# Scans that begin from a constant, and the fifth tile's inputs ahead of the second tile's product, in a selective-scan hybrid block

## The chip, the cores and the metric

The kernel runs on one core of one Trainium2 chip, as one launch. The metric is the device time of that launch in microseconds (us). Engines go by their names in the profile: PE is TensorE, DVE is VectorE, ACT is ScalarE, POOL is GpSimd, SP is SyncE, which issues the DMAs. A difference of some 0.2% is about what a measurement of this kernel can tell from none.

## The reference

The input is x, 8 images of 96 channels, 64 x 64. Layer 0 is a state-space block with a convolutional side: layer norm, a projection to 192 channels and a gate z, a depthwise convolution, then four selective scans (row-wise and column-wise windows, each forwards and backwards) with 16 states to a channel, summed, normed, gated and projected, and a channel-attention part. Layer 1 is attention without softmax and a feed-forward network with fp8 rounding. The part that the change touches is the scan, over l = 4096 positions for each image, direction k, channel d and state n:

```python
def step(hst, inp):
    u_i, dt_i, b_i, c_i = inp
    dA = jnp.exp(dt_i[..., None] * A)
    hst = dA * hst + (dt_i * u_i)[..., None] * b_i[:, :, None, :]
    y = jnp.einsum('bkdn,bkn->bkd', hst, c_i)
    return (hst, y)
h0 = jnp.zeros((bb, k, d, n), u.dtype)
_, ys = lax.scan(step, h0, (u_t, dt_t, b_t, c_t))
return ys.transpose(1, 2, 3, 0) + D[None, :, :, None] * u
```

The names: dA is the decay, dt_i * u_i * b_i the input, hst the state, c_i what the state is multiplied with.

## The kernel before

**Units and tiles.** The scans are cut into 256 units: 8 images x 4 sequences (`order` 0 to 3, a window direction and a scan direction) x 8 chunks of T = 512 positions. A unit is worked in 24 slots, six tiles of G = 4 slots (`TILES`: state group g of 0, 1, channel block j of 0, 1, 2). A slot is one scan over 128 partitions (64 channels x 2 halves of the states) and 512 positions. The state at the end of a chunk goes on to the next unit of its sequence through a column of the tile `carry` (24 columns, one for each slot); the first unit of a sequence (`u.start`) begins from 0.0.

**What a slot runs.** ScalarE makes the decay of the slot two ahead, exp(delta * a), into one of four PSUM banks "da" (`decays(q + 2)`, line 1123). GpSimd has made the inputs of a whole tile beforehand, b * du, 128 x 2048, into a buffer "hb" of six (`inputs`, line 998). VectorE scans (line 1195), with `col`, a pointer to a column of `carry`, as the initial value, or with the constant 0.0. Then comes the product with C, in one of two ways:

- a *banked* slot writes its scan over the decay in PSUM, VectorE makes the product behind the next scan (line 1201) into hb, and ScalarE copies the last state from PSUM to `carry` (line 1202);
- in the other slots the scan writes over the inputs in hb, ScalarE copies the last states of the tile in one instruction (line 1207), and GpSimd makes the product of those slots in place (`outputs`, line 1004).

`BANKED` says how many slots of each of the six tiles are banked: (4, 0, 4, 0, 4, 2), or (4, 0, 4, 0, 4, 3) in image 0 and in the second to fourth sequence of the other images. So tiles 0, 2 and 4 are VectorE's, tiles 1 and 3 GpSimd's, and tile 5 is shared.

PE sums the products over the states by matmuls with `halves` (`sums`, line 1024), ScalarE empties the sums (`gather`), and SP stores them.

**The order.** All engines run in program order, and the order is written out by hand: `plan` says in which slot each step is issued (`put(slot, f, ...)`). Of those the change touches `inputs(u, n + 2)` at slot 4n + 1 (for n of 4 and 5 the next unit's first two tiles), and `sums` of tiles 0 and 1 from slot 13 on. Beside them stand `outputs` of tile 5 of the unit before (slot 0), of tile 1 (8) and tile 3 (16); `step_sizes`, which makes delta and delta * u (its products on GpSimd at slots 12 and 16, line 980); `spread`, `states`, `fetched_dt`, `fetched_u` and `fetched_pair`, which are DMAs on SP. The loads of b and c (`states`, two buffers each) come at slots 7, 10, 15 and 20. In every slot `advance` also runs one step of the side streams: the front part of the next image and the back part of the image before, with their own matmuls, evictions on ScalarE, table loads (line 275) and products on VectorE (lines 450, 465, 653 and others).

**Waits.** A decay needs its bank back: from the product and the carry copy of a banked slot, or from the scan of another. hb of tile n comes back when PE has summed it. `outputs` waits for its tile's scans and for their carry copy, since it overwrites them. `inputs` waits for b, du and a buffer.

Of the kernel before, what the change touches and what calls it, by code (L numbers as in the profile page):

```python
# [9 lines left out]
F32 = mybir.dt.float32  # L10
# [3 lines left out]
ALU = mybir.AluOpType  # L14
# [8 lines left out]
T = 512  # L23
NC = L // T
G = 4
# [5 lines left out]
SPREAD = 5  # L31
HB = 6

BANKED = ((4, 0, 4, 0, 4, 2), (4, 0, 4, 0, 4, 3))

HOLD = 3
LAND = 11
# [6 lines left out]
def kernel(ctx: ExitStack, tc: tile.TileContext, a, out):  # L44
# [8 lines left out]
    nc = tc.nc  # L53
    P = 128
# [8 lines left out]
    def bank(tag, name):  # L63
        return psum.tile([P, T], F32, tag=tag, name=name, bufs=BANKS[tag])
# [630 lines left out]
    def in_turn(stages, k, settle):  # L695

        for stage, cs in stages:
            yield from stage(k, cs)
            if settle:
                yield from settled()  # L700
# [12 lines left out]
    def drained(*streams, beside=()):  # L713
        while any(s.on for s in streams):
            tick()
            for s in (*streams, *beside):
                s.run()

    def all_issued():
        drained(Stream(iter((HOLD + 1,))))  # L720
# [12 lines left out]
    units, images = [], []  # L733
    for b in range(out.shape[0]):

        s = {"b": b, "done": set(), "live": b + 1 == out.shape[0], "pairs": (1, 0) if b else (0, 1)}
        images.append(s)
        for order, (pair, back) in enumerate((p, k) for p in s["pairs"] for k in range(2)):
            for i in range(NC):
                u = Unit()  # L740
                u.s, u.pair, u.back, u.k = s, pair, back, pair + 2 * back
                u.c, u.start = (NC - 1 - i if back else i), i == 0
                u.order, u.new, u.i = order, (order, i) == (0, 0), len(units)
                u.bc, u.hb, u.delta, u.du, u.p = {}, {}, {}, {}, {}
                u.banked = BANKED[int(b == 0 or u.i % 32 >= NC)]
                units.append(u)

    TILES = [(g, j) for g in range(2) for j in range(3)]
# [3 lines left out]
    first = front(0, images[0])  # L752
# [170 lines left out]
    sp = scan_pool.enter_context(tc.tile_pool(name="scan", bufs=2))  # L923
# [76 lines left out]
    def outputs(u, n):  # L1000

        lo = u.banked[n]
        hb = u.hb[n][:, lo:, :]
        nc.gpsimd.tensor_tensor(hb, hb, u.bc[1, TILES[n][0]][:, lo:, :], ALU.mult)  # L1004

# [51 lines left out]
    def plan(u, last, nxt, third, fourth):  # L1057

        at = [[] for _ in range(24)]

        def put(slot, f, *args):
            at[slot].append((f, args))

        if last:
            put(0, outputs, last, 5)
            for m in range(2):
                put(m, sums, last, (3, 4), 2 + m)
            for m in range(2):
                put(3 + m, sums, last, (5,), m)
            put(3, gather, last, 0)  # L1070
            put(7, states, u, 1, 1)
            put(7, gather, last, 1)
        for n in range(6):
            to = (u, n + 2) if n < 4 else (nxt, n - 4)
            if to[0]:
                put(4 * n + 1, inputs, *to)
        if third and u.i % 2:
            put(16, step_sizes, (nxt, third), 5)
        put(8, outputs, u, 1)
        put(16, outputs, u, 3)  # L1080
        for m in range(4):
            put(13 + m, sums, u, (0, 1), m)
            if m < 2:
                put(18 + m, sums, u, (2,), m)
                put(22 + m, sums, u, (3, 4), m)
        put(18, before, u)
        if nxt:
            put(0, spread, nxt, 0, (0, 1))
            put(1, spread, nxt, 1, (0, 1))
            put(10, states, nxt, 0, 0)  # L1090
            put(15, states, nxt, 1, 0)
            put(20, states, nxt, 0, 1)
            if u.i % 2 == 0:
                put(15, spread, nxt, 0, (2,))
                put(16, spread, nxt, 1, (2,))
        if third:
            if third.i < NC:
                put(0, fetched_dt, third)
            put(5, fetched_u, third)
            for i, slot in enumerate((6, 8, 9, 10, 11, 12)):  # L1100
                put(slot, step_sizes, (third,), i)
            if u.i % 2:
                for i, slot in enumerate((9, 11, 12, 13, 15)):
                    put(slot, step_sizes, (nxt, third), i)
                put(17, spread, nxt, 0, (2,))
                put(18, spread, nxt, 1, (2,))
            elif u.i + 3 < len(units):
                put(21, fetched_pair, third, units[u.i + 3])
        if fourth and fourth.i >= NC:
            put(14, fetched_dt, fourth)  # L1110
        return at

    def at_index(i):
        return units[i] if 0 <= i < len(units) else None

    def decays(q):

        if q >= 24 * len(units):
            return
        u, (n, m) = units[q // 24], divmod(q % 24, G)  # L1120
        g, j = TILES[n]
        da[q] = bank("da", "da")
        nc.scalar.activation(  # L1123
            da[q], u.delta[j], AF.Exp, scale=a_neg[:, u.k, j, g * G + m : g * G + m + 1]
        )

    da, kept, side, carry, product = {}, [], [], None, None
    for u in units[:2]:
        fetched_dt(u)
    fetched_u(units[0])  # L1130
# [10 lines left out]
    inputs(units[0], 0)  # L1141
    inputs(units[0], 1)
    decays(0)
    decays(1)
    for i in range(6):
        step_sizes(units[1:2], i)

    def advance(n):

        tick()  # L1150
        for st in side[:]:
            st.run()

    for u in units:
        last, nxt, third, fourth = (at_index(u.i + d) for d in (-1, 1, 2, 3))
        if u.new:
            drained(*side)
            b = u.s["b"]
            side = []
            if b == 0:  # L1160
                half_done.pace = 1.0
                side += [Stream(behind(kit_2, pairs[3:])), half_done]
            else:
                side.append(Stream(chain((SETTLE,), in_turn(back_end(b - 1, last.s), kit_b, False))))
            if b == 0:
                pass
            elif b + 1 < out.shape[0]:
                side.append(Stream(in_turn(front(b + 1, images[b + 1]), kit_f, True), PACE))
            else:
                final = back_end(b, u.s)  # L1170
                last_kit = back_kit(None, "f0", True, kit_f)
                side.append(Stream(final[0][0](last_kit, range(1, NC)[::-1])))
        if u.i == pairs[2] - 2:
            drained(half_done, beside=side[:1])
            side[1] = Stream(in_turn(front(1, images[1]), kit_f, True), PACE * (1 - u.i / 32))
        if u.i == pairs[3] - 2:
            drained(side[0])
        if fourth and fourth.new:
            drained(*side[-1:])
            all_issued()  # L1180
        if u.start:
            carry = sp.tile([P, 24], F32, tag="carry", name="carry")
        todo = plan(u, last, nxt, third, fourth)
        for slot in range(24):
            n, m = divmod(slot, G)
            g, j = TILES[n]
            q, hb, first_at = 24 * u.i + slot, u.hb[n], 0 if u.back else T - 1
            col = carry[:, 8 * j + g * G + m : 8 * j + g * G + m + 1]
            while kept:
                kept.pop(0)()  # L1190
            decays(q + 2)
            d = da.pop(q)
            banked = m < u.banked[n]
            dd, x = (d[:, ::-1], hb[:, m, ::-1]) if u.back else (d, hb[:, m, :])
            nc.vector.tensor_tensor_scan(dd if banked else x, dd, x, 0.0 if u.start else col, ALU.mult, ALU.add)  # L1195
            if product:
                product()
                product = None
            if banked:
                def product(d=d, x=hb[:, m, :], c=u.bc[1, g][:, m, :], col=col, at=first_at):  # L1200
                    nc.vector.tensor_tensor(x, d, c, ALU.mult)  # L1201
                    kept.append(lambda: nc.scalar.copy(col, d[:, at : at + 1]))  # L1202
            elif m == G - 1:
                lo = 8 * j + g * G
                kept.append(
                    lambda c=carry[:, lo + u.banked[n] : lo + G].unsqueeze(2), h=hb[:, u.banked[n] :, :], at=first_at:
                    nc.scalar.copy(c, h[:, :, at : at + 1])  # L1207
                )
            for f, args in todo[slot]:
                f(*args)  # L1210
            place[0] = slot
            advance(slot)
    place[0] = None
    if product:
        product()
# [87 lines left out]
```

## Time and profile before

| what | value |
|---|---|
| time, median of 3 runs (lowest to highest) | 10,763.39 us (10,757.55 to 10,774.28) |
| the profiled execution: time; its span | 10,764.72 us; 10,763.0 us |
| instructions | 97,608 |
| busy in the span, PE; DVE; ACT; POOL | 8,423.7; 10,158.1; 7,397.8; 10,118.0 us |
| mean granted TensorE clock | 0.841 |
| DMA | 2,253 MB, mean 209 GB/s, 0.87 of the 16 engines busy during the scans |
| inputs on POOL, L998, 128 x 2048 | 1536, mean 4,546 ns |
| products on POOL, L1004: 2048; 1024; 512 elements wide | 512, 4,539 ns; 56, 2,362 ns; 200, 1,291 ns |
| decays on ACT, L1123 | 6144, mean 689 ns |
| carry copies on ACT, L1202; L1207 | 3784, 157 ns; 768, 195 ns |

How to read it: a busy time is a union, so where instructions of one engine overlap (the next one's start with the last one's end) the sum of their durations is more than the busy time, and the distance from start to start says what one costs. The scans run from 176 to 10,537 us of the span; what lies before is the front part of image 0, and what lies behind is the back part of the last image. In a group of the profile the columns are line, engine, operation, output <- inputs with shapes and type, count, busy us, mean ns of one, and the engine's idle time just before them with what ended most of it.

### The profile page before, as it was taken

To read this page: it belongs to the slowest core of one execution; us is meant where nothing else is said; L and a number is where in the kernel's file an instruction comes from. 1 tells how busy PE (TensorE), PEld (TensorE's weight loads), DVE (VectorE), ACT (ScalarE), POOL (GpSimd) and SP (SyncE) were. 2 spreads that over 40 slices of the span, in tenths; PEclk is the share of its full clock that TensorE was granted. 3 is DMA by queue.
4 is the path that set the end of the run, shared out by engine and by line. 5 is a ranking of instruction groups with operands and counts; after the bars stand their busy time and mean duration, and the time that the engine had idled before them with its cause. 6 is when DMAs were issued, how large, how long until landed. Compare 5 with 4: busy or idle time off the path is not lost. (4 is left out here: it accounts for less than half of the span.)

```text
span 10763.0 us, 97608 instructions
## 1 busy us (share of the span) xinstructions
PE 8423.7 (78%) x23270; PEld 2274.2 (21%) x23270; DVE 10158.1 (94%) x11126; ACT 7397.8 (69%) x15154; POOL 10118.0 (94%) x2782
## 2 busy tenths in 40 slices
PE   7777668886788867888688886888768887677677
PEld 2121112221122211222122221222112221111112
DVE  3999999999999999999999999999999999999993
ACT  4666666777676776777767776677766767666674
POOL 3999999999999999999999999999999999999991
PEclk8888788987889878998789887898778987778788
DMA  6888888998889988898888988889888898888883
GB/s 148 208 205 209 200 209 214 226 226 200 215 216 227 227 193 220 216 231 219 201 218 214 237 212 202 217 220 237 198 211 218 219 235 200 202 203 210 208 214 94
DMA packets 1095381, 2253.29 MB, mean 209 GB/s; under 512 B 435993, under 2 KB 436698, under 8 KB 963731
## 3 DMA queue, kind: packets, MB, share of 16 engines
q1 hardware_dynamic: 1094803, 2247.05, 84.5%
q8 instruction: 184, 3.01, 0.1%
q14 instruction: 394, 3.23, 0.1%
HBM read 1507.14 MB, written 336.69 MB: 171 GB/s over the span
## 5 line engine op out<-in xcount | busy, mean ns | idle before, releaser
L998 POOL TENSOR_TENSOR hb<-b,du 128x2048 f32<-128x2048 f32 x1536 | 6952.6, 4546 | 6.1 <-DMA du<-ua 5.2
L1024 PE MATMUL p<-hb,halves 128*64 128x512 f32 x12288 | 3713.8, 707 | 1053.0 <-POOL hb L1004 562.6
L1123 ACT ACTIVATE da<-delta,w_a_logs 128x512 f32<-128x512 f32 x6144 | 4164.3, 689 | 541.5 <-DVE hb L1195 447.5
L1195 DVE TENSOR_TENSOR_SCAN da<-da,carry,hb 128x512 f32<-128x512 f32 x3311 | 4164.0, 1274 | 90.7 <-ACT carry L1202 37.0
L1004 POOL TENSOR_TENSOR hb<-hb,c 128x2048 f32<-128x2048 f32 (+2 forms) x768 | 2714.3, 3534 | 222.3 <-ACT carry L1207 203.0
L1195 DVE TENSOR_TENSOR_SCAN hb<-da,carry,hb 128x512 f32<-128x512 f32 x2065 | 2547.0, 1265 | 1.8
L1201 DVE TENSOR_TENSOR hb<-da,c 128x512 f32<-128x512 f32 x3784 | 2534.0, 670 | 1.8 <-DMA c<-xd 0.9
L1202 ACT COPY carry<-da 128x1 f32<-128x1 f32 x3784 | 593.8, 157 | 2054.5 <-DVE hb L1201 2045.1
L1024 PEld LDWEIGHTS p<-hb,halves 128*64 128x64 f32 x12288 | 904.8, 157 | 3697.8 <-issue 1876.0
L313 PE MATMUL conv<-f0im,taps 97*128 97x512 f32 (+1 forms) x2088 | 867.7, 655 | 37.2 <-ACT f0pre L369 32.2
L1195 DVE TENSOR_TENSOR_SCAN da<-da,hb 128x512 f32<-128x512 f32 x473 | 566.1, 1214 | 28.0 <-POOL hb L998 26.6
L963 PE MATMUL dt<-dts,dt_w 7*128 7x512 f32 (+1 forms) x1024 | 485.9, 742 | 92.3 <-ACT carry L1207 36.2
L980 POOL TENSOR_TENSOR ua<-nat,ua 128x512 f32<-128x512 f32 x256 | 329.9, 1289 | 170.9 <-DVE nat L977 161.8
L313 PEld LDWEIGHTS conv<-f0im,taps 97*128 97x128 f32 (+1 forms) x2088 | 256.4, 173 | 588.2 <-issue 508.8
L1207 ACT COPY carry<-hb 128x4 f32<-128x4 f32 (+2 forms) x768 | 149.7, 195 | 302.1 <-DVE hb L1195 293.7
L1195 DVE TENSOR_TENSOR_SCAN hb<-da,hb 128x512 f32<-128x512 f32 x295 | 346.8, 1205 | 1.7 <-ACT carry L1202 1.7
L259 PE MATMUL var<-f1e,ones_c 96*96 96x512 f32 x350 | 225.6, 731 | 121.8 <-ACT f1e L256 68.5
L253 PE MATMUL ctr<-f1e,cen_c 96*96 96x512 f32 x402 | 218.1, 649 | 86.1 <-ACT f1e L592 34.2
L977 DVE SCALAR_TENSOR_TENSOR nat<-dt,nat 128x512 f32<-128x512 f32 x384 | 258.0, 672 | 17.9 <-ACT nat L975 12.7
L975 ACT ACTIVATE nat<-nat,one 128x512 f32<-128x512 f32 x384 | 271.8, 708 | 0.1
L497 PE MATMUL cab<-f1im,cab_w 97*32 97x512 f32 x1044 | 256.0, 603 | 12.5 <-DMA f1im<-xld 7.1
L275 ACT ACT_TABLE_LOAD x193 | 247.6, 1283 | 4.1 <-PEq L1292 0.8
(430 smaller groups left out, 7586.0 us busy)
## 6 DMA issues: line engine op xcount, KB each, us to landing
b<-xd SPq DMA_DIRECT2D x1024, 512.0 KB
c<-xd SPq DMA_DIRECT2D x1024, 512.0 KB
delta<-nat SPq DMA_DIRECT2D x1536, 128.0 KB
du<-ua SPq DMA_DIRECT2D x1024, 128.0 KB
y<-yt SPq DMA_DIRECT2D x512, 256.0 KB
u<-y SPq DMA_DIRECT2D x384, 256.0 KB
ua<-u SPq DMA_DIRECT2D x256, 256.0 KB
du<-ub SPq DMA_DIRECT2D x512, 128.0 KB
```

The costliest lines, as they stand in the source:

```text
L313: nc.tensor.matmul(ps, taps[:, t, lo : lo + n], im[:, r0 + dy : r0 + dy + 8, dx : dx + HW], start=t == 0, stop=t == 8,)
L963: nc.tensor.matmul(ps, dt_w.rearrange("r j d -> r (j d)")[32 * w.k : 32 * w.k + R + 1, d], w.dts, start=True, stop=True)
L975: nc.scalar.activation(u.nat, u.nat, AF.Ln, bias=one)
L977: nc.vector.scalar_tensor_tensor(u.nat, u.ps, 0.0, u.nat, ALU.max, ALU.add)
L980: nc.gpsimd.tensor_tensor(x, u.nat, x, ALU.mult)
L998: nc.gpsimd.tensor_tensor(hb, u.bc[0, g], u.du[j].unsqueeze(1).to_broadcast([P, G, T]), ALU.mult)
L1004: nc.gpsimd.tensor_tensor(hb, hb, u.bc[1, TILES[n][0]][:, lo:, :], ALU.mult)
L1024: nc.tensor.matmul(ps, halves, u.hb[n][:, i, :], start=TILES[n][0] == 0 and m == 0, stop=False, skip_group_check=True)
L1123: nc.scalar.activation(da[q], u.delta[j], AF.Exp, scale=a_neg[:, u.k, j, g * G + m : g * G + m + 1])
L1195: nc.vector.tensor_tensor_scan(dd if banked else x, dd, x, 0.0 if u.start else col, ALU.mult, ALU.add)
L1201: nc.vector.tensor_tensor(x, d, c, ALU.mult)
L1202: kept.append(lambda: nc.scalar.copy(col, d[:, at : at + 1]))
```

## The change

- The initial value of a scan is a constant: 0.0 at the start of a sequence as before, and 1.0 otherwise. In its place ScalarE multiplies the first decay of each slot (the last column in a backward sequence) by the carried state, right behind the exponential that made the decay. With an initial value of 1.0 the scan's first state is then dA * carry + input. The tile `carry` hangs on the unit (`u.carry`), since the decays of a unit's first two slots are made while the unit before still runs.
- `BANKED` becomes (4, 0, 4, 0, 4, 3) and (4, 0, 4, 0, 4, 4); the second now holds only in the even units of those that had it. Where all of tile 5 is banked, `outputs` has nothing to do for it, and nor has the tile's carry copy of line 1207.
- The slots of `inputs` go from 1, 5, 9, 13, 17, 21 to 1, 5, 6, 11, 18, 21, so tile 4's inputs stand ahead of tile 1's `outputs` in GpSimd's order; the sums of tiles 0 and 1 start at slot 14 instead of 13.

```diff
--- before.py
+++ after.py
@@ -31,7 +31,7 @@
 SPREAD = 5
 HB = 6
 
-BANKED = ((4, 0, 4, 0, 4, 2), (4, 0, 4, 0, 4, 3))
+BANKED = ((4, 0, 4, 0, 4, 3), (4, 0, 4, 0, 4, 4))
 
 HOLD = 3
 LAND = 11
@@ -742,7 +742,7 @@
                 u.c, u.start = (NC - 1 - i if back else i), i == 0
                 u.order, u.new, u.i = order, (order, i) == (0, 0), len(units)
                 u.bc, u.hb, u.delta, u.du, u.p = {}, {}, {}, {}, {}
-                u.banked = BANKED[int(b == 0 or u.i % 32 >= NC)]
+                u.banked = BANKED[int((b == 0 or u.i % 32 >= NC) and u.i % 2 == 0)]
                 units.append(u)
 
     TILES = [(g, j) for g in range(2) for j in range(3)]
@@ -1000,6 +1000,8 @@
     def outputs(u, n):
 
         lo = u.banked[n]
+        if lo == G:
+            return
         hb = u.hb[n][:, lo:, :]
         nc.gpsimd.tensor_tensor(hb, hb, u.bc[1, TILES[n][0]][:, lo:, :], ALU.mult)
 
@@ -1073,13 +1075,13 @@
         for n in range(6):
             to = (u, n + 2) if n < 4 else (nxt, n - 4)
             if to[0]:
-                put(4 * n + 1, inputs, *to)
+                put((1, 5, 6, 11, 18, 21)[n], inputs, *to)
         if third and u.i % 2:
             put(16, step_sizes, (nxt, third), 5)
         put(8, outputs, u, 1)
         put(16, outputs, u, 3)
         for m in range(4):
-            put(13 + m, sums, u, (0, 1), m)
+            put(14 + m, sums, u, (0, 1), m)
             if m < 2:
                 put(18 + m, sums, u, (2,), m)
                 put(22 + m, sums, u, (3, 4), m)
@@ -1123,8 +1125,15 @@
         nc.scalar.activation(
             da[q], u.delta[j], AF.Exp, scale=a_neg[:, u.k, j, g * G + m : g * G + m + 1]
         )
-
-    da, kept, side, carry, product = {}, [], [], None, None
+        if not u.start:
+            u.carry = units[u.i - 1].carry
+            first = da[q][:, T - 1 : T] if u.back else da[q][:, 0:1]
+            nc.scalar.mul(first, first, state(u.carry, j, g, m))
+
+    def state(carry, j, g, m, n=1):
+        return carry[:, 8 * j + g * G + m : 8 * j + g * G + m + n]
+
+    da, kept, side, product = {}, [], [], None
     for u in units[:2]:
         fetched_dt(u)
     fetched_u(units[0])
@@ -1179,31 +1188,30 @@
             drained(*side[-1:])
             all_issued()
         if u.start:
-            carry = sp.tile([P, 24], F32, tag="carry", name="carry")
+            u.carry = sp.tile([P, 24], F32, tag="carry", name="carry")
         todo = plan(u, last, nxt, third, fourth)
         for slot in range(24):
             n, m = divmod(slot, G)
             g, j = TILES[n]
             q, hb, first_at = 24 * u.i + slot, u.hb[n], 0 if u.back else T - 1
-            col = carry[:, 8 * j + g * G + m : 8 * j + g * G + m + 1]
             while kept:
                 kept.pop(0)()
             decays(q + 2)
             d = da.pop(q)
             banked = m < u.banked[n]
             dd, x = (d[:, ::-1], hb[:, m, ::-1]) if u.back else (d, hb[:, m, :])
-            nc.vector.tensor_tensor_scan(dd if banked else x, dd, x, 0.0 if u.start else col, ALU.mult, ALU.add)
+            nc.vector.tensor_tensor_scan(dd if banked else x, dd, x, 0.0 if u.start else 1.0, ALU.mult, ALU.add)
             if product:
                 product()
                 product = None
             if banked:
-                def product(d=d, x=hb[:, m, :], c=u.bc[1, g][:, m, :], col=col, at=first_at):
+                def product(d=d, x=hb[:, m, :], c=u.bc[1, g][:, m, :], col=state(u.carry, j, g, m), at=first_at):
                     nc.vector.tensor_tensor(x, d, c, ALU.mult)
                     kept.append(lambda: nc.scalar.copy(col, d[:, at : at + 1]))
             elif m == G - 1:
-                lo = 8 * j + g * G
+                lo = u.banked[n]
                 kept.append(
-                    lambda c=carry[:, lo + u.banked[n] : lo + G].unsqueeze(2), h=hb[:, u.banked[n] :, :], at=first_at:
+                    lambda c=state(u.carry, j, g, lo, G - lo).unsqueeze(2), h=hb[:, lo:, :], at=first_at:
                     nc.scalar.copy(c, h[:, :, at : at + 1])
                 )
             for f, args in todo[slot]:
```

## The prediction

> **What bounds the kernel now.** First the page's busy shares and slices, then the stretch of the scans alone (176 to 10,537 us; the columns after its length are PE, PEld, DVE, ACT, POOL, granted clock, DMA share, GB/s):
>
> ```profile
> PE 8423.7 (78%) x23270; PEld 2274.2 (21%) x23270; DVE 10158.1 (94%) x11126; ACT 7397.8 (69%) x15154; POOL 10118.0 (94%) x2782
> ...
> DVE  3999999999999999999999999999999999999993
> ACT  4666666777676776777767776677766767666674
> POOL 3999999999999999999999999999999999999991
> ```
> ```profile
> 176.00:10537.00 10361.00, 8108.87 (x22408) 2163.15 (x22408) 10083.65 (x10955) 7234.59 (x14903) 10098.15 (x2749) 0.84 0.87 214
> ```
>
> Over 10,361 us VectorE is idle 277 us and GpSimd 263; both are full, side by side. ScalarE has 3,126 us free. The chain that ended last covers only the last few hundred us and says nothing of the scans. The groups and, by form, the small products on GpSimd:
>
> ```profile
> L1195 DVE TENSOR_TENSOR_SCAN da<-da,carry,hb 128x512 f32<-128x512 f32 x3311 | 4164.0, 1274 | 90.7 <-ACT carry L1202 37.0
> ...
> L1195 DVE TENSOR_TENSOR_SCAN hb<-da,carry,hb 128x512 f32<-128x512 f32 x2065 | 2547.0, 1265 | 1.8
> L1201 DVE TENSOR_TENSOR hb<-da,c 128x512 f32<-128x512 f32 x3784 | 2534.0, 670 | 1.8 <-DMA c<-xd 0.9
> L1202 ACT COPY carry<-da 128x1 f32<-128x1 f32 x3784 | 593.8, 157 | 2054.5 <-DVE hb L1201 2045.1
> ...
> L1195 DVE TENSOR_TENSOR_SCAN da<-da,hb 128x512 f32<-128x512 f32 x473 | 566.1, 1214 | 28.0 <-POOL hb L998 26.6
> ...
> L1195 DVE TENSOR_TENSOR_SCAN hb<-da,hb 128x512 f32<-128x512 f32 x295 | 346.8, 1205 | 1.7 <-ACT carry L1202 1.7
> ```
> ```profile
> L1004 POOL TENSOR_TENSOR hb<-hb,c 128x512 f32<-128x512 f32 x200 | 258.2, 1291 | 20.4 <-ACT carry L1207 18.9 <-DMA du<-ua 0.6 <-DMA f1x<-td 0.6
> ...
> L1004 POOL TENSOR_TENSOR hb<-hb,c 128x1024 f32<-128x1024 f32 x56 | 132.3, 2362 | 4.2 <-ACT carry L1207 4.0
> ```
>
> A scan that begins from a carry takes 60 ns more than one that begins from 0.0, with either output. Durations overlap, so I checked on VectorE's timeline that the 60 ns is real time, once where scans carry and once where a sequence begins:
>
> ```profile
> 5011.34 1.27 DVE L1195 TENSOR_TENSOR_SCAN da<-da,carry,hb 128x512 f32<-128x512 f32 x1
> 5012.53 0.67 DVE L1201 TENSOR_TENSOR hb<-da,c 128x512 f32<-128x512 f32 x1
> 5013.12 1.27 DVE L1195 TENSOR_TENSOR_SCAN da<-da,carry,hb 128x512 f32<-128x512 f32 x1
> ...
> 5027.63 1.22 DVE L1195 TENSOR_TENSOR_SCAN da<-da,hb 128x512 f32<-128x512 f32 x1
> 5028.76 0.67 DVE L1201 TENSOR_TENSOR hb<-da,c 128x512 f32<-128x512 f32 x1
> ```
>
> Start to start, the scan costs 1.19 us with a carry and 1.13 without, and a product 0.59. Last, the waits inside the stretch (total, times, longest):
>
> ```profile
> DVE da L1195 <- POOL hb L998: 62.9, 67, 6.9
> DVE f1x L450 <- ACT f1e L449: 55.9, 32, 4.2
> DVE da L1195 <- ACT carry L1202: 37.0, 19, 3.2
> ```
> ```profile
> POOL hb L1004 <- ACT carry L1207: 195.1, 158, 3.0
> ```
>
> All of VectorE's waits that ScalarE ends add up to 178 us. GpSimd's main wait is for tile 1's scans (and tile 5's) before their product with C.
>
> **The change part by part.** (1) *Constant start.* 3311 + 2065 = 5376 scans lose 0.06 us: **-322 us** on VectorE.
>
> (2) *More products on VectorE.* 200 units have 15 and 56 have 14 (sum 3784, the count of L1201). After, the 100 even ones of those 200 have 16 and the other 156 have 15: 3940. 156 more at 0.59 us: **+92 us**. GpSimd loses 56 x (2.36 - 1.29) + 100 x 1.29 = 189 us and stands at 9,909. With its waits other than those for scans (263 - 195 = 68) it needs 9,977, which is 384 below today: GpSimd stops being a bound.
>
> (3) *The multiply on ScalarE*, 5376 times, directly behind its exponential and reading what that wrote. The trace has no such instruction. Bounds: an exponential (691 ns) is followed by an independent one 624 ns after its start, while a dependent pair (L246, L247) leaves 32 ns after the end: the exponential grows by 691 + 32 - 624 = 99 ns. The multiply itself, start to next start: at least 56 ns (a one-column copy before an independent copy, L1202 to L1207); at most its whole duration with a gap, taken from the nearest activation with a pointer operand, 244 + 32 = 276 ns:
>
> ```profile
> L568 ACT ACTIVATE gate<-ca,w_ca_b x8: 244/244/257, 2121.6 to 10647.9; 96x1 f32<-96x1 f32 x8
> ```
>
> That row's own start-to-next-start is 144 ns, and what follows a multiply is mostly independent, as there; I take it. Per scan 0.155 to 0.375, taken 0.243 us; 5376 x 0.243 = 1,306 us, ScalarE's idle 3,126 goes to some 1,710 (20 us of further carry copies and 95 us of shorter span included).
>
> Is it hidden? The exponential is issued two scans ahead; in the trace a decay is ready a median 2.5 us before its scan, but under 0.97 us in one of ten and under 0.35 in one of fifty, after bursts such as the two table loads and the silu. There VectorE will stand. Two counts: waits grow as the idle share shrinks, 178 x (3,126/1,710 - 1) = +147; or, going through the trace in order, adding 0.243 us to ScalarE's lateness at each exponential, taking each of its recorded gaps off, and pushing VectorE where the lateness exceeds the lead recorded: +184. I take **+165 us**; the bounds of the multiply make it +88 to +320. Behind the multiply stand the carry copies and the streams' evictions, and PE waits for those banks; that matters only where VectorE reads such a result, which is in both counts.
>
> The Trainium skill (ScalarE: Activation LUTs, What ACT_TABLE_LOAD costs) gives an activation 186 ns plus 93 for a pointer operand, back-to-back overlap 93. The trace has less: the exponential with its pointer 689 against 618 without one (L973), so 71 ns. By the page the multiply spaces 187 ns instead of 144, an estimate that would make the sum about -60 instead of -95. Its Rules for kernel authors speak against this change outright: multiplications belong on VectorE.
>
> (4) *Order on GpSimd.* inputs(u,4) goes ahead of outputs(u,1), inputs(u,5) from slot 13 to 11, inputs(nxt,0) from 17 to 18. None issues a DMA. outputs(u,1), which waited on average 195.1/158 = 1.2 us, now comes some 4.5 - 1.2 = 3.3 us later; its readers are PE's sums (moved one slot, 1.1 to 1.7 us, later) and SP's load of the next c at slot 15. PE is 78% busy, and c is due nine slots, over 10 us, later: nothing, with a cover of that size; were it gone, it would come back as VectorE waiting for L998. The buffer that inputs(u,4) takes is freed by sums at slot 1, five slots earlier. The gain is that a freer GpSimd is later less often: I take half of VectorE's 62.9 us, **-31** (0 to -63).
>
> Sum: -322 + 92 + 165 - 31 = -96; the profiled execution's own 10,764.7 (span 10,763.0; 1.3 over the median of the runs) becomes **10,670 us**.
>
> **Rivals.** *ScalarE keeps up*: its slack of 3,126 us speaks for it, the short leads against. -322 + 92 - 63 = -293, 10,470; with the multiply at its lower bound -322 + 92 + 88 - 31 = -173, 10,590.
>
> *ScalarE becomes the bound*, the slower side: in tiles 1 and 3 no product stands between scans, a slot is 1.13 us, and 0.62 + 0.24 leaves 0.27 for evictions. With the multiply fully exposed at 0.375 us the idle left is about 1,100, waits grow by 320, and the sum is +90: 10,855. It decides from about 0.34 us by the first count, 0.28 by the second. For it: the fullest units already hold 36 us of ScalarE work in about 42.
>
> *The gain and the new waits cancel*, at about 0.3 us per scan: 10,763.
>
> *The constant is not the reason* for the shorter scan but its value 0.0 or an empty carry: then +92 + 165 - 31, 10,990. Against it: the difference is 60 ns in both groups.
>
> **How the numbers follow.** Forecast (10,590 to 10,740) 0.48, ScalarE keeps up 0.17, cancelled 0.12, ScalarE the bound 0.20, constant no cheaper 0.03. Faster by over 0.2% (21 us, about what can be told from no change): 0.65; within 0.12; slower 0.23. The range, 10,540 to 10,810, leaves out the best of the second case and the worst of the two slower ones.
>
> **What would show it.** Scans all near 1,214 and 1,205 ns; L1201 x3940; products on GpSimd x512 of 2048, x156 of 512, none of 1024; ScalarE busy near 8,600 us; its multiply spaced 0.14 us; VectorE's waits for ScalarE near 340; outputs(u,1) without its wait. It is wrong if a scan keeps 1,270 ns, if the multiply with its exponential adds over 0.28 us, or if VectorE's waits for L998 grow.

## The result, and the profile after

The changed kernel takes 10,806.7 us (median of 6 runs, 10,793.0 to 10,807.0) beside 10,758.3 for the kernel before (median of 6, the three of the table among them): ratio of the means 1.0039, 95% interval 1.0026 to 1.0052. It is slower by 0.4%, where 10,670 was forecast, and the time lies at the upper end of the range.

The busy line and the slices of three engines in the page after:

```profile
PE 8553.4 (79%) x23270; PEld 2304.1 (21%) x23270; DVE 9941.3 (92%) x11282; ACT 8582.6 (79%) x20586; POOL 9938.8 (92%) x2682
...
DVE  3999999999999999999999999999999999999993
ACT  5787777888778887888888888788887888777784
POOL 3999999999999999999999999999999999999991
```

The stretch of the scans alone (columns as before):

```profile
176.00:10580.00 10404.00, 8240.86 (x22410) 2194.02 (x22412) 9866.86 (x11111) 8418.11 (x20334) 9918.02 (x2649) 0.83 0.87 213
```

VectorE has 217 us less to do than before (10,084 to 9,867) and GpSimd 180 less (10,098 to 9,918), near the 230 and 189 that were worked out. Yet the stretch is 43 us longer: VectorE's idle time went from 277 to 537 us, GpSimd's from 263 to 486. ScalarE has 1,184 us more to do. The groups that answer to those shown of before:

```profile
L1203 DVE TENSOR_TENSOR_SCAN da<-da,hb 128x512 f32<-128x512 f32 x3940 | 4735.6, 1215 | 238.6 <-ACT da L1131 110.0
...
L1209 DVE TENSOR_TENSOR hb<-da,c 128x512 f32<-128x512 f32 x3940 | 2641.6, 670 | 1.6 <-DMA c<-xd 0.6
L1203 DVE TENSOR_TENSOR_SCAN hb<-da,hb 128x512 f32<-128x512 f32 x2204 | 2586.7, 1206 | 35.7 <-ACT da L1131 23.8
...
L1131 ACT ACTIVATE da<-da,carry 128x1 f32<-128x1 f32 x5376 | 1269.6, 236 | 174.6
```

Every scan is now at 1,215 or 1,206 ns, and there are 3940 products. The multiply (L1131) takes 236 ns, and the 174.6 us of idle time before 5376 of them are 32 ns each, between the end of the exponential that it depends on and its own start. From an exponential's start to its multiply's 724 ns pass, from the multiply's to the next instruction's 159; an exponential alone takes 624. So the multiply costs 724 + 159 - 624 = 0.259 us a scan. And the waits, of VectorE and of GpSimd (total, times, longest):

```profile
DVE da L1203 <- ACT da L1131: 110.0, 113, 3.4
DVE da L1203 <- ACT carry L1210: 66.1, 30, 3.5
DVE f1ln L597 <- ACT var L247: 46.6, 37, 4.1
DVE f1pre L450 <- ACT f1pre L449: 41.3, 42, 1.2
DVE da L1203 <- POOL hb L998: 40.7, 30, 6.9
```
```profile
POOL hb L1006 <- ACT carry L1215: 205.0, 141, 9.3
POOL ub L980 <- DVE nat L977: 170.1, 68, 6.9
POOL hb L998 <- PE p L1026: 74.3, 36, 3.1
```

All of VectorE's waits that ScalarE ends now add up to 431 us (178 before): for decays, but also for the side streams' evictions and norms. GpSimd, with less to do, stands and waits: most of all for VectorE's scans and ScalarE's copy of their last states (205 us), and for VectorE's step sizes (170).

### The profile page after: what moved, and what is told of

Its sections match the earlier page's. It is cut to its first block, busy times and chain, and to the rows that moved or that the text cites. A ratio compares the mean times of both kernels' runs of the same rounds, so it can differ in the third digit from the quotient of the medians.

```text
span 10805.2 us, 103262 instructions
## 1 busy us (share of the span) xinstructions
PE 8553.4 (79%) x23270; PEld 2304.1 (21%) x23270; DVE 9941.3 (92%) x11282; ACT 8582.6 (79%) x20586; POOL 9938.8 (92%) x2682
## 5 line engine op out<-in xcount | busy, mean ns | idle before, releaser
L998 POOL TENSOR_TENSOR hb<-b,du 128x2048 f32<-128x2048 f32 x1536 | 6930.1, 4543 | 82.5 <-PE p L1026 74.3
L1203 DVE TENSOR_TENSOR_SCAN da<-da,hb 128x512 f32<-128x512 f32 x3940 | 4735.6, 1215 | 238.6 <-ACT da L1131 110.0
L1125 ACT ACTIVATE da<-delta,w_a_logs 128x512 f32<-128x512 f32 x6144 | 4237.8, 691 | 454.2 <-DVE hb L1203 353.5
L1006 POOL TENSOR_TENSOR hb<-hb,c 128x2048 f32<-128x2048 f32 (+1 forms) x668 | 2525.6, 3781 | 209.9 <-ACT carry L1215 205.0
L1209 DVE TENSOR_TENSOR hb<-da,c 128x512 f32<-128x512 f32 x3940 | 2641.6, 670 | 1.6 <-DMA c<-xd 0.6
L1203 DVE TENSOR_TENSOR_SCAN hb<-da,hb 128x512 f32<-128x512 f32 x2204 | 2586.7, 1206 | 35.7 <-ACT da L1131 23.8
L1131 ACT ACTIVATE da<-da,carry 128x1 f32<-128x1 f32 x5376 | 1269.6, 236 | 174.6
L980 POOL TENSOR_TENSOR ub<-nat,ub 128x512 f32<-128x512 f32 x128 | 164.5, 1285 | 178.9 <-DVE nat L977 170.6
L497 PE MATMUL cab<-f1im,cab_w 97*32 97x512 f32 x1044 | 292.0, 678 | 9.4 <-DMA f1im<-xld 7.2
L657 PE MATMUL ff<-f1x,q_w 96*128 96x512 fp8e5 x174 | 88.8, 510 | 238.7 <-DVE f1x L653 125.0
L534 PE MATMUL cab<-f1m,cab_w 96*96 96x512 f32 x348 | 208.9, 728 | 59.4 <-ACT f1e L543 33.9
```

The source lines that it names most:

```text
L497: nc.tensor.matmul(ps[at : at + 32, :], cab1_w[:, t, :], k.im.t[:, 8 * q + dy : 8 * q + dy + 8, dx : dx + HW], start=t == 0, stop=t == 8, ...
L980: nc.gpsimd.tensor_tensor(x, u.nat, x, ALU.mult)
L998: nc.gpsimd.tensor_tensor(hb, u.bc[0, g], u.du[j].unsqueeze(1).to_broadcast([P, G, T]), ALU.mult)
L1125: nc.scalar.activation(da[q], u.delta[j], AF.Exp, scale=a_neg[:, u.k, j, g * G + m : g * G + m + 1])
L1131: nc.scalar.mul(first, first, state(u.carry, j, g, m))
```

## The experiments

The theory after the result: ScalarE's multiply makes ScalarE late, and VectorE gives back in waits more than it gained. The rivals: GpSimd's new order does the harm, or the new split of the products.

**The change without the multiply.** `no_mul` is the changed kernel with the multiply removed, so the carried state is left out.

```diff
-            first = da[q][:, T - 1 : T] if u.back else da[q][:, 0:1]
-            nc.scalar.mul(first, first, state(u.carry, j, g, m))
```

> The changed kernel without ScalarE's multiply: every scan but the first of a sequence begins from the constant 1.0 and the carried state is left out. If ScalarE's multiply is what the time went to, VectorE's waits for ScalarE fall from some 420 us back to about 180 and the time is 10,480 to 10,600. If the new order on GpSimd or the products moved to VectorE did it, the waits stay and the time is over 10,720.

Measured 10,589 us (0.984 of before, interval 0.9825 to 0.9855). The multiply costs 10,807 - 10,589 = 218 us. The time is within the first range, though VectorE's waits for ScalarE are 241 us and not some 180. Its stretch of the scans:

```profile
176.00:10361.70 10185.70, 8181.89 (x22408) 2175.16 (x22408) 9845.36 (x11111) 7247.14 (x14957) 9916.44 (x2649) 0.84 0.89 217
```

VectorE is as busy as in the changed kernel, but idle 340 us and not 537.

**The parts by themselves.** `scan_only` has the constant start with the multiply, and the old split and order; `rest_only` the new split and order, and the pointer start; `old_order` is the change with the old order; `old_bank` the change with the old split; `order_only` and `bank_only` are the kernel before with one part alone. Their edits, each against the changed kernel, are made of these three:

```diff
# the old start (rest_only, order_only, bank_only), with the multiply removed
-0.0 if u.start else 1.0, ALU.mult, ALU.add)
+0.0 if u.start else state(u.carry, j, g, m), ALU.mult, ALU.add)
# the old order (scan_only, old_order, bank_only)
-put((1, 5, 6, 11, 18, 21)[n], inputs, *to)
+put(4 * n + 1, inputs, *to)
-put(14 + m, sums, u, (0, 1), m)
+put(13 + m, sums, u, (0, 1), m)
# the old split (scan_only, old_bank, order_only)
-BANKED = ((4, 0, 4, 0, 4, 3), (4, 0, 4, 0, 4, 4))
+BANKED = ((4, 0, 4, 0, 4, 2), (4, 0, 4, 0, 4, 3))
-u.banked = BANKED[int((b == 0 or u.i % 32 >= NC) and u.i % 2 == 0)]
+u.banked = BANKED[int(b == 0 or u.i % 32 >= NC)]
```

> Constant start and multiply alone; the split of the products, GpSimd's order and the slots of the sums as before. VectorE loses 320 us of work, GpSimd none (10,098 busy). If ScalarE's lateness is the cause: 10,720 to 10,800, within 0.5% of the kernel before. If the reorder or the split did the harm: under 10,690.

> Split and order of the change, the scans still beginning from the pointer, no multiply. VectorE gains 92 us of work. If these parts are harmless apart from that work: 10,760 to 10,850. If the reorder costs time by itself: over 10,870.

> The changed kernel with GpSimd's inputs at slots 1, 5, 9, 13, 17, 21 and the sums from slot 13 again. If ScalarE's lateness is the cause, within 30 us of the changed kernel's 10,807. If the new order is the cause, 10,680 to 10,760; if the order is what makes the rest bearable, over 10,840.

> The changed kernel with the split of the products as before (VectorE 92 us less, GpSimd 189 us more). If VectorE with its waits is the bound: 10,700 to 10,760. If a GpSimd of 10,098 us busy is the bound again: 10,760 to 10,810.

> The kernel before with the new order on GpSimd and the sums from slot 14, nothing else. VectorE's work is as before. If the order's worth is that GpSimd stops standing still for tile 1's scans (195 us) and so feeds VectorE in time: 10,690 to 10,740. If an order alone is worth no more than beside the rest (21 us with the new split): 10,735 to 10,760.

> The kernel before with the new split of the products alone: VectorE 92 us more, GpSimd 189 us less. If VectorE with its waits is the bound, the 92 us come out nearly whole: 10,820 to 10,870. If GpSimd was the bound: under 10,760.

With the kernel before (10,764 to 10,766 beside these runs) and the changed kernel, all eight combinations are there:

| order | split | pointer start | constant start and multiply |
|---|---|---|---|
| old | old | 10,764 (before) | 10,792 (1.0027; 1.0017 to 1.0036) |
| old | new | 10,812 (1.0043; 1.0026 to 1.0060) | 10,828 (1.0057; 1.0042 to 1.0072) |
| new | old | 10,721 (0.9958; 0.9944 to 0.9973) | 10,739 (0.9975; 0.9965 to 0.9984) |
| new | new | 10,776 (1.0012; 1.0002 to 1.0021) | 10,807 (the change) |

Each part has the same sign wherever it stands. The new order is worth 21 to 53 us. The new split costs 36 to 68. The constant start with its multiply costs 16 to 31. The smallest of these are no more than the 0.2% that can be told from nothing, so that those signs rest on the four together; and the changed kernel was timed in another series, beside 10,758 and not 10,764 for the kernel before, so differences to it may be off by some 6 us. `scan_only`, `rest_only` and `order_only` fell within the first range named for them. The order was a gain, so that rival falls; the split does harm of its own, which the theory had missed. `old_order` came out 21 us over the changed kernel, inside the 30 us named for the theory, with the sign of an order that helps; `old_bank` fell within the expectation that VectorE with its waits is the bound, `bank_only` 8 us below it.

What the order and the split do can be seen in GpSimd. The stretch and GpSimd's wait for scans and their copies, first with the new order alone, then with the new split alone (there with VectorE's wait for GpSimd's inputs):

```profile
176.00:10495.40 10319.40, 8198.17 (x22419) 2176.24 (x22420) 10065.20 (x10955) 7235.12 (x14904) 10097.17 (x2749) 0.84 0.87 214
```
```profile
POOL hb L1006 <- ACT carry L1213: 59.7, 62, 8.7
```
```profile
176.00:10582.20 10406.20, 8131.86 (x22408) 2159.32 (x22408) 10171.91 (x11111) 7264.02 (x14955) 9916.38 (x2649) 0.83 0.86 213
```
```profile
POOL hb L1006 <- ACT carry L1213: 433.1, 214, 7.9
DVE da L1201 <- POOL hb L998: 12.8, 7, 7.0
```

With the order, GpSimd's wait for scans falls from 195 to 60 us: tile 1's product, with 167 us the most of it before, waits no more. Other waits of GpSimd grow (for VectorE's step sizes from 28 to 83 us, for PE from 1 to 53), and the stretch falls by 42. With the split, VectorE gets 88 us more to do and GpSimd 182 less. That shortens VectorE's waits for GpSimd's inputs by 50 us (63 to 13), and GpSimd's own wait grows from 195 to 433 us, in 285 of which the tile's scans had not ended: the stretch grows by 45.

**Where the multiply stands.** `tiles024` has constant start and multiply only in the twelve slots of tiles 0, 2 and 4, `tiles13` only in the eight of tiles 1 and 3; all else is as in the change.

```diff
-            first = da[q][:, T - 1 : T] if u.back else da[q][:, 0:1]
-            nc.scalar.mul(first, first, state(u.carry, j, g, m))
+            if n in (0, 2, 4):
+                first = da[q][:, T - 1 : T] if u.back else da[q][:, 0:1]
+                nc.scalar.mul(first, first, state(u.carry, j, g, m))
-0.0 if u.start else 1.0, ALU.mult, ALU.add)
+0.0 if u.start else 1.0 if n in (0, 2, 4) else state(u.carry, j, g, m), ALU.mult, ALU.add)
```

> The changed kernel, but only the twelve slots of tiles 0, 2 and 4 (a product between scans, 1.7 us a slot) begin from the constant and have the multiply; the others begin from the pointer again. If every multiply costs the same wherever it stands, half of the 217 us goes and half of the 186 us of gain: 10,780 to 10,800. If the multiplies in the short slots of tiles 1 and 3 are what makes ScalarE late: 10,660 to 10,740.

> The counterpart: only the eight slots of tiles 1 and 3 (1.13 us a slot) begin from the constant and have the multiply. Same cost wherever it stands: 10,780 to 10,790. If the short slots are what makes ScalarE late: 10,800 to 10,860.

Measured 10,753 and 10,766. Both expectations missed: the first time lies between the two ranges named, the second is under both. Against the same split and order with the pointer start (10,776), 2688 multiplies come out 23 us faster, 1792 come out 9, and all 5376 lose 31. The 23 are just at the 0.2% that can be told from nothing, the 9 below it. So it isn't the short slots: with the multiply in them alone nothing is lost. Gain and loss nearly cancel all through: in the traces VectorE's work falls by 0.054 to 0.057 us for each multiply, and its idle time grows by 0.053 (`tiles024`), 0.055 (`tiles13`) and, with all of them, 0.061.

Neither kernel has the multiply in the four slots of tile 5, so the two don't make up the whole. Whether the number of multiplies or those slots turn the balance is not shown. What the traces do show is that of the 330 us by which VectorE's idle time grows with all of them, 50 stand in tile 5's slots, about their share of the slots.

**Queue time or latency.** `dummy_mul` has, in place of the multiply, one that no scan waits for.

```diff
-            first = da[q][:, T - 1 : T] if u.back else da[q][:, 0:1]
-            nc.scalar.mul(first, first, state(u.carry, j, g, m))
+            nc.scalar.mul(scrap, state(u.carry, j, g, m), state(u.carry, j, g, m))
```

> The kernel without the multiply (10,589), with a multiply of a carry column into a scratch column in its place: ScalarE is as often busy, but no scan waits for it and it doesn't read what the exponential wrote (the carried state is left out as there). If ScalarE's time in its queue is the cost, in proportion to the spacing (some 0.15 of 0.26 us): 10,690 to 10,740. If the cost is that a decay is ready later by the multiply's latency: under 10,640.

Measured 10,688 us, 2 below what was named for queue time and 98 above the kernel without a multiply. Its group on ScalarE:

```profile
L1130 ACT ACTIVATE scrap<-carry 128x1 f32<-128x1 f32 x5376 | 1510.3, 281 | 0.4
```

Start to start it is spaced 185 ns and the exponential before it 627 in place of 624, so 0.188 us a scan, 73% of the real one, for 45% of its 218 us. ScalarE's queue time alone, with no scan waiting for the result, costs about half. The other 120 us are the further 0.07 us a scan and the decay's being ready later; these two were not separated. How far ahead ScalarE runs shows both: from the moment when a decay is ready to its scan, the traces have a median of 2.5 us in `rest_only`, 2.4 in `no_mul`, 2.0 in `dummy_mul` and 1.6 in the changed kernel, and in one of ten under 0.97, 0.90, 0.63 and 0.30 us.

**A version from this.** `half_old_bank` joins what the runs favoured: the new order, the old split, and the constant start in tiles 0, 2 and 4 (the edits of `tiles024` and of the old split).

> New order, old split, and the constant start with its multiply in tiles 0, 2 and 4 alone: ScalarE some 700 us less busy than with all of them, VectorE about 160 us less than before. If the waits grow faster than ScalarE's load: 10,650 to 10,715, under both kernels and under the 10,739 with all of them. If GpSimd's 10,098 us are the bound there: 10,715 to 10,745.

Measured 10,714 us: 0.9953 of before, interval 0.9938 to 0.9968, the fastest of the kernels that bring in the carried state, though its interval overlaps that of the order alone (10,721). Both are faster than the kernel before and the changed one. It lies at the border of the two ranges named, so it doesn't decide between them.

**The carry without ScalarE's multiplies.** `columns` brings it in beforehand: three exponentials of eight columns a unit for the first decays, their products with the carry and their sums into the inputs' first column on VectorE.

```diff
-            nc.scalar.mul(first, first, state(u.carry, j, g, m))
...
+            nc.scalar.activation(
+                u.heads[:, j].rearrange("p g m -> p (g m)"), a_neg[:, u.k, j, :], AF.Exp,
+                scale=u.delta[j][:, at : at + 1],
+            )
...
+        nc.vector.tensor_tensor(t, t, was, ALU.mult)
...
+        nc.vector.tensor_tensor(h, h, u.heads[:, j, g, :].unsqueeze(2), ALU.add)
```

> New order, old split, every scan from the constant 0.0, and the carry brought in another way: ScalarE makes the first decays of a unit in three instructions of eight columns, VectorE multiplies them with the carry (three small products a unit) and adds them to the first column of each tile's inputs (six small sums). ScalarE gets 672 instructions in place of 5376 (some 125 us in place of 1,390), VectorE loses 320 us and gains 2,016 small ones at 0.06 to 0.12 us (120 to 240). If ScalarE's load is what ate the gain: 10,600 to 10,690, under the order alone (10,721). If a faster VectorE is worth nothing beside a GpSimd of 10,098 us: 10,700 to 10,740.

Measured 12,649 us, 1.175 of before: a miss. The 2,016 small instructions were not 0.06 to 0.12 us. By form, on VectorE:

```profile
L1081 DVE TENSOR_TENSOR hb<-hb,heads 128x4 f32<-128x4 f32 x1344 | 1230.1, 915 | 0.0
L1074 DVE TENSOR_TENSOR heads<-heads,carry 128x4 f32<-128x4 f32 x224 | 938.7, 4191 | 0.0
```

A sum of four columns took 915 ns on average. The timelines of VectorE and of GpSimd, one after the other, say why:

```profile
5002.32 0.13 DVE L1081 TENSOR_TENSOR hb<-hb,heads 128x4 f32<-128x4 f32 x1
...
5008.64 4.30 DVE L1081 TENSOR_TENSOR hb<-hb,heads 128x4 f32<-128x4 f32 x1
5012.87 1.22 DVE L1236 TENSOR_TENSOR_SCAN da<-da,hb 128x512 f32<-128x512 f32 x1
```
```profile
4996.65 4.52 POOL L998 TENSOR_TENSOR hb<-b,du 128x2048 f32<-128x2048 f32 x1
5003.95 4.51 POOL L1006 TENSOR_TENSOR hb<-hb,c 128x2048 f32<-128x2048 f32 x1 [2.78 <-ACT carry L1248]
5008.41 4.52 POOL L998 TENSOR_TENSOR hb<-b,du 128x2048 f32<-128x2048 f32 x1
```

At 5002.32 GpSimd is idle and the sum takes 0.13 us. At 5008.64 GpSimd has just begun a product that ends at 5012.93, and the sum ends at 5012.94. The run therefore says nothing on whether ScalarE's load ate the gain; it says that this way of taking it off is closed.

## Why the prediction was wrong

**(1) Constant start, -322.** The work is right: 60 ns a scan, and VectorE 310 us less busy between `rest_only` and `no_mul`. Its worth is not. Even with no multiply the time falls by 10,776 - 10,589 = 187 us (by the profiles 177, since the profiled execution of `rest_only` was 10 us under its median). VectorE's stretch with new split and order, and the pointer start:

```profile
176.00:10537.90 10361.90, 8253.93 (x22407) 2223.03 (x22408) 10155.32 (x11110) 7263.83 (x14954) 9913.19 (x2648) 0.83 0.87 213
```

It is idle 207 us there and 340 in `no_mul`. The two waits that grow most, in `rest_only` and then in `no_mul`:

```profile
DVE f1ln L597 <- ACT var L247: 17.6, 20, 1.3
DVE da L1201 <- POOL hb L998: 8.8, 2, 7.1
```
```profile
DVE da L1201 <- POOL hb L998: 69.1, 58, 6.9
DVE f1ln L597 <- ACT var L247: 46.9, 26, 4.7
```

By releaser, its waits for GpSimd grow from 9 to 69 us and those for ScalarE from 180 to 241, with the work of both unchanged: a faster VectorE uses up the leads by itself.

**(2) Split, +92.** VectorE's 88 us more are as counted; in time they are 36 to 68. The difference is what GpSimd's 189 us less bought, for which the sum had no term: VectorE's waits for its inputs fell by some 50 us (63 to 13 with the old order, 61 to 9 with the new). Little more was to be had: before the change VectorE waited 63 us for GpSimd and GpSimd 195 for VectorE's scans and their copies, as two lines of the prediction showed.

**(3) The multiply, and the step that failed.** Its price was nearly right, 0.259 us and not 0.243. What failed is the step from work to waits: the sum took the constant start's -322 whole as time, and the only new waits in it were the +165 for the multiply. From `rest_only` to the changed kernel VectorE's idle time grows by 537 - 207 = 330 us, twice that: 133 come with the faster VectorE alone, for which the sum had nothing, and 197 with the multiply. Both counts started from the waits and leads that the old VectorE had left. In time, the prediction had -322 + 165 = -157 for start and multiply, and the runs have -187 + 218 = +31: 188 us worse than forecast, 135 of them in the worth of the constant start and 53 in the multiply. Split (+55 with the new order in place, not +92) and order (-43, not -31) came out 49 better; the rest, 139 us, is the way from the forecast's -96 to the -43 + 55 + 31 = +43 of the runs.

**(4) Order, -31.** The size is near, -43 alone and -21 beside the rest, but by luck. The gain was to be half of VectorE's wait for GpSimd's inputs, and that hardly moved in `order_only` (63 to 61 us); it was GpSimd's wait for scans that went. VectorE's idle time falls there from 277 to 254 us; its waits that fell are two of a side stream (L450 for L449 56 to 34, L465 for PE 19 to 10). How the order shortens those, and the stretch by 42 us, was not traced further.

**The rivals.** The time lies between "the gain and the new waits cancel" (10,763) and "ScalarE becomes the bound" (10,855). For start and multiply by themselves, 16 to 31 us, the first comes nearest, at 0.259 us a scan and not at about 0.3; the split adds the rest. ScalarE was late, not full: it had 1,986 us of the stretch free. The constant did shorten the scan, so the last rival fell. None of the three signs named for being wrong came (scans take 1,215 and 1,206 ns, the multiply adds 0.259 us, VectorE's waits for L998 fell from 63 to 41): all three asked for the price of the parts, none for what a faster VectorE would wait. Of the signs for being right, VectorE's waits for ScalarE (431 us where 340 were expected) gave the miss away.

## What to carry to other kernels

When work leaves a full engine for one that is 69% busy but runs only a few instructions ahead, ask first what the shorter work alone would be worth: here 187 of 310 us, before the other engine got anything to do. What then comes on top counts from the shorter leads: the multiply cost 218 us, though the engine that got it still had 1,986 us of the stretch free. Where two engines look equally full, let their waits for each other say which one may be given work; and when a change has several parts, run them apart: here one was a gain and two were losses.

## What the runs showed of the hardware

- VectorE's small product or sum with both operands in SBUF waited for GpSimd: 1,268 of the 2,016 in `columns` took over 0.3 us, up to 11.7, and these ended some 24 ns after the end of a GpSimd instruction. The other 748 (the shortest took 0.127) began while GpSimd was idle or in the last 0.3 us of its instruction, but for one that began at the same moment. The Trainium skill (SBUF — State Buffer, SBUF: two separate sides) has the rule: a VectorE instruction with two SBUF inputs and a GpSimd one that reads SBUF share a port pair that one of them holds for its whole length. The runs agree. The scans and products of this kernel each take one operand from PSUM, and stayed at 1,206 to 1,215 and 670 ns beside a GpSimd that is 92% busy.
- A multiply of one column on ScalarE took 236 ns from PSUM to PSUM (spaced 159) and 281 from SBUF to SBUF (spaced 185). The Trainium skill (ScalarE: Activation LUTs, What ACT_TABLE_LOAD costs) has 186 ns, 93 for a pointer operand and 0.833 an element, so 280 for one column, an estimate from the page, and an overlap of 93 between neighbours: the SBUF form agrees, and the PSUM form of the change was 44 ns cheaper.
